# A two-layer graph-attention kernel: Q, K and V of a group computed one step later, the start of the kernel laid out anew, and a bias added elsewhere

## Chip, core and metric

The kernel runs on one core of one Trainium2 chip. The metric is the device time of one execution in microseconds (us). Names of engines: PE is the matrix engine (PEld its weight loads), DVE the vector engine, ACT the scalar engine, POOL the GpSimd engine, SP the engine that issues nearly all DMAs here. Each engine works through its own queue in order.

## What is computed

There are 128 graphs of 128 nodes with 512 features, `x[128,128,512]`, and an adjacency matrix `adj[128,128,128]` of zeros and ones for each. All is float32. Layer 0 is masked attention with 8 heads of 64 features and an output projection, layer 1 a graph attention with one head whose softmax runs over the other axis:

```python
q, k, v = x @ Wq + bq, x @ Wk + bk, x @ Wv + bv            # (128, 128, 512) each
a = softmax(where(adj > 0, q_h @ k_h.T / 8, -1e9))         # for each of 8 heads
x = layernorm(x + relu(concat_h(a @ v_h) @ Wo + bo))
Wh = x @ W                                                 # layer 1
e = leaky(Wh @ a[:512] + (Wh @ a[512:]).T, 0.2)            # (128, 128) for each graph
att = softmax(where(adj > 0, e, -9e15), axis=1)
out = layernorm(x + leaky(att @ Wh, 0.2))
```

bk has no effect on a softmax over the keys and is not used by the kernel.

## The kernel before

**Products.** Every large product is cut into 2 x 2 blocks and done by Winograd's form of Strassen's scheme (`strassen`): seven block products p1, p5, p6, p2, p7, p4, p3 in place of eight. Right-hand blocks (weights) are summed once at the start by four DVE subtractions (`right_blocks`, L134-137), left-hand blocks for each product by four POOL operations (`left_blocks`, L289-292). Three PSUM accumulators y, w, x take the seven products: p1, p6, p7, p4 go into y, and ACT reads y out after p1 (t0), p6 (t2), p7 (t3) and p4, before the next product adds to it; p5 and p3 go into w, with a DVE addition that needs t3 between them; p2 goes into x, and DVE adds t0 to it.

**Groups.** Q, K and V are computed for a group of four graphs at once (`products`, `group_product`): 3 x 7 = 21 block products of 8 matmul instructions on line 361 (tiles st_y, st_w, st_x), in a fixed order in which the three chains overlap. Three PSUM banks "a", "b", "c" are handed from chain to chain, so a first use of a bank by one chain waits until the chain before has read it out. The sums of V's weights are written to DRAM once and fetched into a ring of three buffers for each group (wv_n, L402). Wo and W1 are used for pairs of graphs (`project_o` in odd steps, `project_w` in even ones, L442, tiles p_y, p_w, p_x).

**Steps.** The order on all five engines is written by hand: a loop over steps t (one graph each) issues the scores of graph t (lg, L486, 16 matmuls), its softmax (DVE maxima L495 and L501, eight exponentials L507 and eight divisions L521 on ACT), a round trip through DRAM and a DVE transpose (paT, L536), the attention product of graph t-1 (p_oT, L549) and its copy to SBUF (L561), the projections of earlier graphs, and layer 1 of graph t-7. `group()` is called five times in a step, after the maxima, after the transpose, after the first four divisions, after the attention product, and at the end; each call issues one of the 21 products (the last call of the fourth step what is left). So the products fill PE while the softmax runs on ACT and DVE.

**Before the first scores.** The loop begins at t = -4. Before it the kernel loads the bias rows (L110, L111, on ACT's queue) and turns them (L114-116), loads graphs 0 to 3 one by one with four DMAs each (L257, on SP's queue), Wq in 16 DMAs (ACT's queue), Wk and Wv in 16 each (SP's), scales Wq's four blocks (L151), and transposes the graphs (L262); the last transpose of a group also issues the POOL sums xS. Group g's products are issued in steps 4g-4 to 4g-1, so those of group 0 in steps -4 to -1, where nothing else runs.

**Wo and W1.** Wo is loaded in step 0 and combined in one piece at the end of step 1: the four subtractions, then `bo_b` += bv @ Wo by ten PE products (p_bo, L184-189), and the split of the bias row into three bf16 rows (L197-204). W1 is loaded in step 2 and combined at the end of step 4: 16 dot products with the attention vector on DVE (wa_scr, L229), eight tiny additions (L240) and the four subtractions.

Of the kernel before, what the change touches and what calls it, by code (L numbers as in the profile page):

```python
# [8 lines left out]
F32 = mybir.dt.float32  # L9
# [8 lines left out]
GROUP = 4  # L18
EPS = 1e-5
# [5 lines left out]
def kernel(  # L25
# [16 lines left out]

# [67 lines left out]
    nc.scalar.dma_start(b_rows[:NC, :], bq.rearrange("(c p) -> c p", p=P))  # L110
    nc.scalar.dma_start(b_rows[NC:, :], bv.rearrange("(c p) -> c p", p=P))  # L111
    b_cols = const.tile([P, 2, NC], F32, name="b_cols")
    p_b = psum("p_b")
    nc.tensor.transpose(p_b[:, : 2 * NC], b_rows, ident[: 2 * NC, : 2 * NC])  # L114
    nc.vector.tensor_scalar_mul(b_cols[:, 0, :], p_b[:, :NC], QSCALE)
    nc.vector.tensor_copy(b_cols[:, 1, :], p_b[:, NC : 2 * NC])

    def weight_blocks(w, t, queue, spread_rows=True):

        b12 = work.tile([P, 2, t[0].shape[-1]], F32, name="b12", tag="z")  # L120
        blocks = {(0, 0): t[0], (1, 0): t[1], (0, 1): b12, (1, 1): t[2]}
        for (k, o), dst in blocks.items():
            if spread_rows:
                rows = w.rearrange("(q k c i) (o f) -> k o q i c f", q=4, k=2, c=2, o=2)
                for q in range(4):
                    queue.dma_start(dst[32 * q : 32 * q + 32, :, :HALF], rows[k, o, q])
            else:
                rows = w.rearrange("(k c p) (o f) -> k o p c f", k=2, c=2, o=2)
                queue.dma_start(dst[:, :, :HALF], rows[k, o])
        return blocks  # L130

    def right_blocks(t, b12):

        nc.vector.tensor_sub(t[4], b12, t[0])  # L134
        nc.vector.tensor_sub(t[6], t[2], b12)
        nc.vector.tensor_sub(t[5], t[2], t[4])
        nc.vector.tensor_sub(t[3], t[1], t[5])
# [7 lines left out]
    def load_wq():  # L145
        t = [wq[:, n] for n in range(7)]
        blocks = weight_blocks(Wq, t, nc.scalar)

        def combine():
            for dst in blocks.values():  # L150
                nc.vector.tensor_scalar_mul(dst, dst, QSCALE)  # L151
            right_blocks(t, blocks[0, 1])

        return combine

    def load_wk():
        t = [wk[:, n] for n in range(7)]
        blocks = weight_blocks(Wk, t, nc.sync)
        return lambda: right_blocks(t, blocks[0, 1])

    def load_wv():
        tiles = [big.tile([P, 2, 2, HALF], F32, name="wv_t", tag="v", bufs=3) for _ in range(3)]
        tiles.append(work.tile([P, 2, 2, HALF], F32, name="wv_t", tag="paT"))
        t = [tiles[n // 2][:, n % 2] for n in range(7)]
        blocks = weight_blocks(Wv, t, nc.sync)

        def combine():
            right_blocks(t, blocks[0, 1])
            for n in range(7):
                nc.sync.dma_start(wv[n], t[n])  # L170

        return combine

    def load_wo():

        t = [wo[:, n] for n in range(7)]
        blocks = weight_blocks(Wo, t, nc.sync, spread_rows=False)
        bo_b = work.tile([P, D], F32, name="bo_b", tag="y")
        nc.sync.dma_start(bo_b, bo.partition_broadcast(P))

        def combine():
            right_blocks(t, blocks[0, 1])
            rows = work.tile([P, NC, P], F32, name="bv_rows", tag="z")
            nc.vector.tensor_copy(rows, b_cols[:, 1, :].unsqueeze(2).to_broadcast([P, NC, P]))  # L184
            p = psum("p_bo")
            parts = [(0, 0, 0), (0, 1, 1), (1, 0, 0), (1, 4, 0), (1, 2, 1)]
            for o, n, k in parts:
                for c in range(2):
                    nc.tensor.matmul(
                        p[:, o * HALF : (o + 1) * HALF],  # L190
                        rows[:, 2 * k + c, :],
                        wo[:, n, c, :],
                        start=o == 0 and n == 0 and c == 0,
                        stop=True,
                        skip_group_check=True,
                    )
            nc.vector.tensor_add(bo_b, bo_b, p)  # L197
            nc.vector.tensor_sub(bo_b[:, HALF:], bo_b[:, HALF:], bo_b[:, :HALF])
            for n in range(3):
                row = slice(32 * n, 32 * n + 1)  # L200
                part = work.tile([P, D], BF16, name="b_part", tag="z")
                nc.vector.tensor_copy(part, bo_b)
                nc.vector.tensor_copy(bias_rows[row, :], part[row, :])
                nc.vector.tensor_sub(bo_b, bo_b, part)

        return combine

    bias_rows = const.tile([96, D], BF16, name="bias_rows")
    nc.gpsimd.memset(bias_rows, 0.0)
    ones = const.tile([96, P], BF16, name="ones")  # L210
    nc.gpsimd.memset(ones, 1.0)

    def load_w1():

        t = [w1[:, n] for n in range(7)]
        blocks = weight_blocks(W1, t, nc.sync)
        a_b = work.tile([P, 2, D], F32, name="a_b", tag="x1T")
        nc.sync.dma_start(
            a_b.rearrange("p s f -> p (s f)"),
            a1.rearrange("f o -> (f o)").partition_broadcast(P),  # L220
        )

        def combine():
            sums = small.tile([P, 2, 2, 2, 2], F32, name="wa", bufs=1)
            for (k, o), block in blocks.items():
                for c in range(2):
                    for s in range(2):
                        scr = work.tile([P, HALF], F32, name="wa_scr", tag="y")
                        nc.vector.scalar_tensor_tensor(  # L229
                            scr,  # L230
                            block[:, c, :HALF],
                            1.0,
                            a_b[:, s, o * HALF : (o + 1) * HALF],
                            op0=ALU.mult,
                            op1=ALU.mult,
                            accum_out=sums[:, s, k, o, c : c + 1],
                        )
            for (k, o), block in blocks.items():
                for c in range(2):
                    nc.vector.tensor_add(  # L240
                        block[:, c, HALF:],
                        sums[:, o, k, 0, c : c + 1],
                        sums[:, o, k, 1, c : c + 1],
                    )
            right_blocks(t, blocks[0, 1])

        return combine
# [19 lines left out]
    def load_x(b):  # L267
        X[b] = spread(x[b])
# [6 lines left out]
    def transpose_x(b):  # L275
# [4 lines left out]
        if j == GROUP - 1:  # L280
            sums = big.tile([P, 3, 2, 2 * P], F32, name="xS")
            XS[g] = left_blocks(XT[g], sums)
# [100 lines left out]
    def products(g):  # L383
# [20 lines left out]
        def fetched(n):  # L404
# [4 lines left out]
            group_product(g, 3 * g, lambda n: wq[:, n], features_first(Q), True, b_cols[:, 0, :]),  # L409
            group_product(g, 3 * g + 1, lambda n: wk[:, n], features_first(K), True),  # L410
# [10 lines left out]
        order = chains[0][:5]  # L421
        for n in range(3):
            if n < 2:
                order.append(chains[n + 1][0])
            order += chains[n][5:]
            if n < 2:
                order += chains[n + 1][1:5]
        return order

    def pair_product(xs, w, add, bias=None):  # L430
# [3 lines left out]
        def multiply(p, n, start):  # L434
# [6 lines left out]
            for kc in range(2):  # L441
# [3 lines left out]
                    w[:, n, kc, :],  # L445
# [95 lines left out]
    def attend(sm):  # L541
# [16 lines left out]
        def copy():  # L558
            if h == 0:
                OT[pair] = work.tile([P, NC, 2 * P], F32, name="oT")  # L560
            nc.scalar.copy(OT[pair][:, :, h * P : (h + 1) * P], p)  # L561
# [157 lines left out]
    combine = {}  # L719
    group_steps = []  # L720
    later = []
    sm = fin = none

    x_turns = [(8,), (8, 9), (9,), ()]
    load_x(0)
    load_x(1)
    combine["wq"] = load_wq()
    load_x(2)
    load_x(3)
    transpose_x(0)  # L730
    transpose_x(1)
    combine["wq"]()
    combine["wk"] = load_wk()
    transpose_x(2)
    transpose_x(3)
    load_x(4)
    combine["wk"]()
    combine["wv"] = load_wv()
    for t in range(-4, B + 9):
        pair_steps = []  # L740
        if t % GROUP == 0 and on(t + 4):
            group_steps = products((t + 4) // GROUP)
# [5 lines left out]
        def group(n=1):  # L748
            for _ in range(min(n, len(group_steps))):
                group_steps.pop(0)()  # L750

# [4 lines left out]
        if on(t + 1):  # L756
            load_mask(t + 1)
        if t == 0:
            combine["wo"] = load_wo()
        if t == 2:  # L760
            combine["w1"] = load_w1()
# [11 lines left out]
        fin.stats()  # L773
        pair()
# [34 lines left out]
        if t == 4:  # L809
            combine["w1"]()  # L810
# [7 lines left out]
        if t == -4:  # L818
            combine["wv"]()
        if t == 1:  # L820
            combine["wo"]()
        group(21 if t % GROUP == GROUP - 1 else 1)
# [41 lines left out]
```

## Time and profile before

| what | value |
|---|---|
| median of 3 runs | 2527.51 us (2526.45 to 2529.57) |
| the profiled execution | 2527.99 us, span of its trace 2526.2 us |
| busy in it: PE, DVE, ACT, POOL | 2445.9, 1809.8, 1355.3, 801.6 us |
| granted PE clock, mean | 0.985 |
| 4 steps in the middle (1000.00 to 1075.30 us) | PE 75.30, DVE 55.41, ACT 42.22, POOL 25.03 us busy |
| scores of step 0 to 6 begin at | 57.64, 68.60, 91.01, 104.59, 124.18, 135.32, 164.47 us |
| scores of step 124 to 127 begin at | 2386.19, 2400.69, 2416.73, 2434.21 us |

In the profile a group of instructions is named by its line, engine and operation and by the tiles that it writes and reads ("st_y<-xT,wq"). The timeline gives start, duration, and in brackets the time for which the engine sat idle before and what released it. The table of waits gives for each waiting engine and line the total, the number and the longest wait.

### The profile page before, as it was taken

How to read it: one execution, taken by the hardware profiler on the slowest of the kernel's cores; microseconds unless marked ns; L12 is line 12 of the kernel's file. 1: busy time of each engine (PE TensorE's matmuls, PEld its weight loads, DVE VectorE, ACT ScalarE, POOL GpSimd, SP SyncE). 2: the span in 40 equal slices, each digit the busy share in tenths (PEclk: the TensorE clock that was granted, in tenths of full speed). 3: DMA queues.
4: the chain of work that ended last, by engine and by line, in shares of the span. 5: the costliest groups of instructions: out<-in, count | busy, mean ns of one | idle time of the engine just before them, and what ended most of it. 6: DMA issues, size and time to landing. Idle time of an engine off the chain costs nothing.

```text
span 2526.2 us, 43418 instructions
## 1 busy us (share of the span) xinstructions
PE 2445.9 (97%) x13717; PEld 2009.6 (80%) x13717; DVE 1809.8 (72%) x3758; ACT 1355.3 (54%) x4801; POOL 801.6 (32%) x1161
## 2 busy tenths in 40 slices
PE   7889999999999999999999999999999999999975
PEld 6778888888888888888888888888888888888753
DVE  4567777777777777777777777777777777777675
ACT  1445555555565565565555555555555555555541
POOL 1132333332333332333333233333233333233232
PEclk9999999999999999999999999999999999999987
DMA  5544554545554545445545444545445545444441
GB/s 169 154 133 150 156 151 157 158 145 162 155 153 150 162 148 158 153 150 159 157 153 159 148 153 152 160 154 157 147 155 153 159 154 155 154 153 147 145 132 46
DMA packets 353350, 379.91 MB, mean 150 GB/s; under 512 B 39640, under 2 KB 257760, under 8 KB 353120
## 3 DMA queue, kind: packets, MB, share of 16 engines
q1 hardware_dynamic: 351824, 376.07, 47.9%
q8 instruction: 110, 1.80, 0.3%
q10 hardware_dynamic: 1296, 1.05, 0.2%
q14 instruction: 120, 0.98, 0.1%
HBM read 240.91 MB, written 136.05 MB: 149 GB/s over the span
## 4 chain that ended last, share of the span: by engine, by line
PE 93%; DVE 3%; ACT 1%; DMA 1%; issue 1%; POOL 0%; SPq 0%; DVEq 0%; ACTq 0%; POOLq 0%
PE st_y L361 26%; PE p_y L442 17%; PE st_w L361 13%; PE p_w L442 8%; PE st_x L361 7%; PE lg L486 5%; PE p_oT L549 5%; PE p_h L683 4%; PE p_x L442 4%; ACT pa L507 1%; PE p_e L654 1%; PE p_e L655 1%; DVE pa L495 0%; DVE wa_scr L229 0%; DVE z L692 0%
## 5 line engine op out<-in xcount | busy, mean ns | idle before, releaser
L575 POOL TENSOR_SCALAR ve<-mv 128x1 f32<-128x1 f32 x256 | 68.7, 268 | 1187.8 <-DVE mv L572 1187.8
L507 ACT ACTIVATE pa<-pa,nmax 128x128 f32<-128x128 f32 x1024 | 400.4, 393 | 25.7 <-DVE nmax L501 22.6
L521 ACT ACTIVATE pa<-pa,rs 128x128 f32<-128x128 f32 x1024 | 333.1, 396 | 0.1
L495 DVE TENSOR_TENSOR pa<-lg,mf 128x512 f32<-128x512 f32 x256 | 164.7, 685 | 71.2 <-PE lg L486 69.1
L338 ACT COPY st_t<-st_y 128x512 f32<-128x512 f32 x192 | 110.4, 575 | 186.7 <-PE st_y L361 186.7
L643 DVE TENSOR_TENSOR wh<-p_w,pr_t 128x257 f32<-128x257 f32 x128 | 54.5, 426 | 211.2 <-ACT pr_t L453 125.1
L486 PEld LDWEIGHTS lg<-kT,qT 64*128 64x128 f32 x2048 | 124.2, 187 | 93.7 <-issue 93.7
L507 ACT ACTIVATION_READ_ACCUMULATOR pa<-pa,nmax 128x1 f32 x1024 | 194.8, 190 | 0.0
L577 POOL TENSOR_TENSOR rstd<-ve,mhalf 128x1 f32<-128x1 f32 x256 | 176.8, 691 | 21.4
L453 ACT COPY pr_t<-p_y 128x256 f32<-128x256 f32 (+1 forms) x384 | 140.8, 367 | 76.8 <-PE p_y L442 76.1
L342 ACT ACTIVATE st_t<-st_y,b_cols 128x256 f32<-128x256 f32 x192 | 80.6, 470 | 177.2 <-PE st_y L361 177.2
L687 ACT COPY z<-p_h 128x512 f32<-128x512 f32 x128 | 75.1, 586 | 181.9 <-PE p_h L683 167.4
L289 POOL TENSOR_TENSOR oS<-oT 128x256 f32<-128x256 f32 x64 | 46.8, 731 | 396.1 <-ACT oT L561 396.1
L536 DVE STREAM_TRANSPOSE paT<-paz 128x1024 f32<-128x1024 f32 x128 | 159.4, 1245 | 4.9 <-DMA paz<-pa_dram 4.2
L501 DVE TENSOR_REDUCE nmax<-pa 128x8 f32<-128x1024 f32 x128 | 156.2, 1220 | 4.4
L561 ACT COPY oT<-p_oT 128x512 f32<-128x512 f32 x128 | 75.1, 586 | 154.9 <-PE p_w L442 151.9
L683 PE MATMUL p_h<-wh,att 128*128 128x512 f32 x256 | 134.0, 605 | 17.5 <-DVE att L674 17.5
L549 PEld LDWEIGHTS p_oT<-paT,v 128*64 128x64 f32 x2048 | 113.4, 140 | 46.3 <-issue 34.5
L486 PE MATMUL lg<-kT,qT 64*128 64x128 f32 x2048 | 148.7, 285 | 0.0
L442 PE MATMUL p_y<-w,x1S 128*128 128x257 f32 x512 | 134.6, 385 | 13.8 <-ACT pr_t L453 13.8
L549 PE MATMUL p_oT<-paT,v 128*64 128x128 f32 x2048 | 144.9, 285 | 1.8 <-DVE rs L517 1.8
L442 PE MATMUL p_y<-wo,oS 128*128 128x256 f32 x512 | 134.5, 386 | 10.2 <-ACT pr_t L453 10.2
(154 smaller groups left out, 6027.0 us busy)
## 6 DMA issues: line engine op xcount, KB each, us to landing
pa_dram<-pa SPq DMA_DIRECT2D x128, 512.0 KB, 2.6
paz<-pa_dram SPq DMA_DIRECT2D x512, 128.0 KB, 2.9
wv_n<-wv SPq DMA_DIRECT2D x224, 256.0 KB, 2.9
xz<-in_x_dram SPq DMA_DIRECT2D x512, 64.0 KB, 2.4
x<-in_x_dram SPq DMA_DIRECT2D x128, 256.0 KB, 3.1
x_dram<-x SPq DMA_DIRECT2D x128, 256.0 KB, 2.3
xz<-x_dram SPq DMA_DIRECT2D x512, 64.0 KB, 2.0
out_dram<-z SPq DMA_DIRECT2D x128, 256.0 KB, 2.0
```

Of the source, the lines that this page charges most:

```text
L361: nc.tensor.matmul(p[:, m, :], lhs, rhs, start=start and m == 0 and kc == 0, stop=True, skip_group_check=True,)
L442: nc.tensor.matmul(p[:, :width], xs[n][:, kc, :], w[:, n, kc, :], start=start and kc == 0, stop=True, skip_group_check=True,)
L453: nc.scalar.copy(t[:, :width], p[:, :width])
L486: nc.tensor.matmul(self.lg[r][:, c, :], q[rows, c, cols], k[rows, c, cols], start=True, stop=True)
L495: nc.vector.tensor_add(by_head[:, r * NC : (r + 1) * NC], self.lg[r].rearrange("p c (b k) -> p c b k", b=4), mf.unsqueeze(1).to_broadcast( ...
L501: nc.vector.tensor_reduce(self.nmax, by_head, AX.XY, ALU.max, negate=True)
L507: nc.scalar.activation(self.pa[:, :, h, :], self.pa[:, :, h, :], AF.Exp, bias=self.nmax[:, h : h + 1], accum_out=self.sums[:, h : h + 1],)
L521: nc.scalar.activation(self.pa[:, :, h, :], self.pa[:, :, h, :], AF.Copy, scale=self.rs[:, h : h + 1])
L536: nc.vector.transpose(self.paT.rearrange("p h (a i) -> p a h i", i=32), self.paz.rearrange("p a (h k) -> p a h k", k=32),)
L549: nc.tensor.matmul(p[r * HD : (r + 1) * HD, c, :], v[:, h * HD : (h + 1) * HD], sm.paT[:, r * NC + c, :], start=True, stop=True,)
L577: nc.gpsimd.tensor_tensor(rstd, ve, mhalf, ALU.pow)
L683: nc.tensor.matmul(p.rearrange("p (o f) -> p o f", o=2), edge.att, wh, start=True, stop=True)
```

## The change

- `products(g)` starts at t = 4g-3 in place of 4g-4, and the loop begins at t = -3. Products 1 to 15 (Q and K whole and V's p1) are issued in the three steps before the group's first scores, V's p5, p6, p2, p7, p4, p3 in the step of those scores. In each chain p3 now comes ahead of p4; in group 0 the first chain runs p1, p2, p5, p6, p7.
- The POOL sums of group g+1 (`sum_x`) are issued early in step 4g. Graphs are loaded and transposed at other steps (`x_turns`), as many in four steps as before.
- Graphs 0 to 3 come as two pairs of four DMAs each and two transposes of 1024 columns; weight blocks in 8 DMAs in place of 16; the blocks have other places in memory (`PLACE`). The bias rows are issued on ACT's queue after Wq, and their PE transpose still stands ahead of the first product.
- bv is added to O^T when it is copied out of PSUM: four activations with a bias column in place of one copy. The product p_bo and what fed it are gone.
- The sums of Wk, Wv, Wo, the bias rows and W1 are a list of small operations ("chores"); each `group()` call issues two after its product. Wo is loaded in step -2, W1 in step -1.

```diff
-            nc.scalar.copy(OT[pair][:, :, h * P : (h + 1) * P], p)
+            for c in range(NC):
+                nc.scalar.activation(
+                    OT[pair][:, c, h * P : (h + 1) * P],
+                    p[:, c, :],
+                    AF.Identity,
+                    bias=b_cols[:, 1, c : c + 1],
+                )
...
-        order = chains[0][:5]
-        for n in range(3):
-            if n < 2:
-                order.append(chains[n + 1][0])
-            order += chains[n][5:]
-            if n < 2:
-                order += chains[n + 1][1:5]
-        return order
+        order = [chains[0][n] for n in ((0, 3, 1, 2, 4) if g == 0 else range(5))]
+        for n in range(2):
+            order += [chains[n + 1][0], chains[n][6], chains[n][5]]
+            order += chains[n + 1][1:5]
+        return order + chains[2][5:]
...
-    x_turns = [(8,), (8, 9), (9,), ()]
...
+    x_turns = [(), (7, 8), (8,), (8,)]
+    xz = load_pair(0, "pa")
+    load_blocks(Wq, columns(wq), nc.scalar)
+    nc.scalar.dma_start(b_rows[:NC, :], bq.rearrange("(c p) -> c p", p=P))
+    nc.scalar.dma_start(b_rows[NC:, :], bv.rearrange("(c p) -> c p", p=P))
+    xz2 = load_pair(1, "paz")
+    load_blocks(Wk, columns(wk), nc.sync)
+    XT[0] = big.tile([P, NC, GROUP * P], F32, name="xT")
...
+    wq_sums = right_blocks(places(wq))
+    scale(0)
+    transpose_pair(0, xz)
+    scale(1)
+    transpose_pair(1, xz2)
+    sum_x(0)
+    scale(2)
+    wq_sums[0]()
+    scale(3)
+    for op in wq_sums[1:]:
+        op()
+    turn_biases()
     load_x(4)
-    combine["wk"]()
-    combine["wv"] = load_wv()
-    for t in range(-4, B + 9):
+    load_x(5)
+    chores += right_blocks(places(wk)) + load_wv()
+    for t in range(-3, B + 9):
         pair_steps = []
-        if t % GROUP == 0 and on(t + 4):
-            group_steps = products((t + 4) // GROUP)
+        if t % GROUP == 1 and on(t + 3):
+            group_steps = products((t + 3) // GROUP)
...
             for _ in range(min(n, len(group_steps))):
                 group_steps.pop(0)()
+            for _ in range(min(CHORES, len(chores))):
+                chores.pop(0)()
...
-        if t == 0:
-            combine["wo"] = load_wo()
-        if t == 2:
-            combine["w1"] = load_w1()
+        if t == -2:
+            load_blocks(Wo, columns(wo), nc.sync, spread_rows=False)
+            more_chores = right_blocks(places(wo)) + load_bias()
+        if t == -1:
+            chores += more_chores
+            more_chores = load_w1()
+        if t == 0:
+            chores += more_chores
...
         fin.stats()
+        if t % GROUP == 0 and on(t + GROUP):
+            sum_x(t // GROUP + 1)
...
-        group(21 if t % GROUP == GROUP - 1 else 1)
+        group(21 if t % GROUP == 0 else 1)
```

`CHORES` is 2. `load_wv` gives as chores one write of a block to DRAM, the four subtractions and six more writes; `load_bias` one subtraction and three splits of three operations; `load_w1` eight pairs of dot products, four pairs of tiny additions and the four subtractions.

## Prediction

> **What bounds the kernel now.** I read the page's chain first, then busy time by stretches, then the waits and the timeline of the first 165 us, and last the end.
>
> ```profile
> PE 93%; DVE 3%; ACT 1%; DMA 1%; issue 1%; POOL 0%; SPq 0%; DVEq 0%; ACTq 0%; POOLq 0%
> ```
>
> The chain runs over PE. Busy time of PE, PEld, DVE, ACT, POOL for four steps early on and in the middle:
>
> ```profile
> 76.80:152.10 75.30, 64.46 (x364) 52.73 (x364) 50.32 (x116) 30.98 (x113) 16.43 (x20) 0.95 0.50 149
> 1000.00:1075.30 75.30, 75.30 (x429) 62.21 (x429) 55.41 (x116) 42.22 (x151) 25.03 (x37) 1.00 0.49 154
> ```
>
> In the middle PE never idles: four steps cost 75.3 us, 18.8 each, whatever the other engines do. Time can only be won before about 165 us, where PE waits, and after 2387. PE's waits of the first 200 us:
>
> ```profile
> PE st_w L361 <- POOL xS L289: 6.6, 1, 6.6
> PE st_w L361 <- DVE qT L379: 5.2, 1, 5.2
> PE st_y L361 <- DMA b<-in_L_gnn_Wq_dram: 5.0, 1, 5.0
> PE p_bo L189 <- DVE bv_rows L184: 3.2, 1, 3.2
> ```
>
> The first PE product starts at 8.3, the second only at 18.7 (behind scaling and sums of Wq, transposes, POOL's xS). Then 19 more run, and the scores of step 0 begin at 57.64. Step 1 takes 22.4 us (68.60 to 91.01) because Wo's lump of DVE and PE work stands in it, step 5 takes 29.2 (135.32 to 164.47) because W1's lump (135.0 to 147.1 on DVE) stands ahead of its maxima:
>
> ```profile
> 83.08 6.27 PE L189 MATMUL p_bo<-wo,bv_rows 128*128 128x256 f32 x20 [3.17 <-DVE bv_rows L184]
> 149.01 3.46 PE L361 MATMUL st_w<-xT,wq 128*128 128x256 f32 x8 [5.20 <-DVE qT L379]
> ```
>
> Prices from rows: a block product 1.73 us (the chain's pitch), scores 1.09, p_oT 1.03, project_o 6.3, project_w 6.1, a DVE sum 0.60, a bias part 1.44, an exponential with its accumulator 0.58, a division 0.295, an ACT copy of a bank 0.59.
>
> **Part 1, to the first scores.** The PE queue begins with the transpose of the bias rows, which now follow Wq's 8 DMAs. By issue alone (0.57 us each, then 1.64 to land) they are there at 7.9. By bytes they come later: ahead of them lie 2 MB (graphs 0 to 3 and Wq), and before moved at most 230 to 242 GB/s in the slices from 4.5 to 9 us, so some 10. I take 10 (bounds 7.9 and 12, the latter by the mean pace to 10.5 us). The page's DMA row for this, of the first 60 us in slices of 1.5:
>
> ```profile
> GB/s 0 133 173 233 230 242 161 231 132 135 142 145 141 131 138 137 136 159 134 133 131 199 378 407 365 325 170 124 150 160 15 0 75 124 150 216 180 262 249 289
> ```
>
> [...]
>
> From 10: p1 cold 3.7 (the row before: 8 matmuls in 3.78), p2 and p5 1.73 each, p6 to 18.9. p5's inputs (POOL's first sum, 1.27 after pair 1's transpose, and one sum of Wq) are due at about 12.5, so the wait of 6.6 goes. Next late is ACT's reading of p6 (0.84 plus hand-over), on which p7 now follows directly: 1.1. p7 ends at 21.8, K's p1 at 23.5. Q's p3 needs p7's DVE addition, and that stands behind Wv's first sums in DVE's queue; Wv is the last of 4.5 MB, there at about 20.8 (240 GB/s and 2 us to land); three sums and two transposes later it is 24.0, the addition 24.7. So p3 starts at 24.8: a wait of 1.3. Q's p4, 28.2; K's p5 waits 1.0 for ACT's copy of p4 (same bank), ends 31; six more products: 41.4. **Scores of step 0 at 41.5** (bounds 39 and 48: a start at 7.9, or Wv and the writes of its sums, which share SP's queue with the fetches, late by 6). That is 16.1 earlier, 10.4 of it because six products are left over.
>
> **Part 2, steps 0 to 5.** The six products of V now stand in steps 0 and 4, where no project_o or project_w fills PE, and they hang on ACT: p7 on the copy of p6, which comes after six exponentials, p4 on the copy of p7, which comes after all divisions. From the scores' end: maxima 2.6, exponentials 3.5, copy 0.6, p7; then two exponentials, eight divisions, cast and copy to 11.4; p4, p3, next scores: 16.2. In step 0 the maxima also stand behind two bias parts, a transpose and a mask (2.6 late): 18.9 us where step 0 before had 10.96. In step 4 bv's activations come before the copy (1.2): 17.3 plus 0.5, where it had 11.1. Each time PE idles some 4 us. Rows on that: after an idle time of 2.17 the next 8 matmuls took 1.99, after 5.20 they took 3.46. The Trainium skill, "TensorE: Matmul & The Clock Gate", section "The HAM clock gate", puts the fall to half rate at an idle window of about 3.4 us; by it each of these gaps would cost up to 1.7 more, by the shorter row nothing. I count 0.5 for step 4, and nothing for step 0, where ACT is later than even a half-rate p7.
>
> Step 1 is like step 0 before: 11.2, as the rest of W1's chores is under 4 us of DVE. Step 2 has Q's p4, then K's p5 on the same bank behind exponentials and four divisions: 14.3. Step 3: 18.3, step 5: 17.8, by PE's work. Sum 18.9 + 11.2 + 14.3 + 18.3 + 17.8 + 17.8 = 98.3 where it was 106.8. **Scores of step 6 at 139.8 in place of 164.47: 24.7 won.** Step 7 has one product less than before: 26.4.
>
> **Part 3, the middle.** p_oT's copy becomes four activations. Nearest rows: one copy of 512 columns 0.586, one activation of 128 from PSUM 0.368, two of 256 in 0.84; so 1.2, 0.6 more in a step, ACT 42 to 45 of 75. It is off PE's path if the hand-overs keep their slack. The two that get tight are Q's p4 to K's p5 in step 4g+2 and K's p4 to V's p5 over the end of step 4g+3 (1.4 us left, by the order of ACT's queue). For the first, ACT's read of the product before and PE's start of the next in such a step:
>
> ```profile
> 2321.14 0.84 ACT L342 ACTIVATE st_t<-st_y,b_cols 128x256 f32<-128x256 f32 x2 [0.67 <-PE st_y L361]
> 2322.93 1.99 PE L361 MATMUL st_x<-xT,wq 128*128 128x256 f32 x8
> ```
>
> 0.9 us is left. K's p3 to the next scores has 4.4 us of other PE work for 0.7 of DVE. POOL's sums (5.1 us) start at about 8 us of step 4g, done before O^T's at 13.8. SP issues as many DMAs in four steps as before. So nothing; bounds 0 and 0.5 us a group each at the two places.
>
> **Part 4, the end.** Step 124 gets the six products that step 0 of the kernel shed. Before it took 14.5, with
>
> ```profile
> 2394.26 1.74 PE L442 MATMUL p_y<-w,x1S 128*128 128x257 f32 x4 [3.06 <-ACT pr_t L453]
> ```
>
> and now costs a full step with V's products, 20.2 (step 123 before: 2365.97 to 2386.19): 5.7 lost. ACT's 0.6 on the last graphs' way to project_o: 0.6 more.
>
> **The sum.** 26.4 - 5.7 - 0.6 = 20.1. The profiled execution's span 2526.2 becomes 2506.1, its 2527.99 us 2507.9; the median shown lies 0.5 below the profiled time, so I say **2508**. A measurement here can tell about 0.2% (5 us) from no change.
>
> **Rivals.** (a) *The V steps stall less and PE starts early*: scores of step 0 at 39, steps 0 and 4 at 13 each, since DVE may get to the maxima sooner: 2.5 + 5.9 + 4.8 more, 2495. For it: only step 0 has the backlog. Against: ACT's order is fixed, and the exponentials before p6's copy alone are 3.5. 0.14. (b) *The start is late*: V's weights go through SP in order with writes, x, Wo and W1, and each wait there holds all behind it; scores of step 0 at 48 and step 0 longer by 3 to 5: 2518. For it: before, SP's queue stood behind the ring of V for 9 us at 42.9. Against: nothing in the new order needs the ring before V's p1. 0.13. (c) *Slower: ACT becomes the bound at the hand-over*. If ACT is as late at the third `group()` as in the steps that have K's p2, where its read began 11.0 us after the scores' start and PE's next product at 12.1, a read of 0.84 leaves 0.2, and bv's 0.6 a step eats that. It decides from 20 / 31 = 0.65 us a group; at 1.0 a group it is 31 us: 2539. Against: ACT idles 33 of 75 us and catches up in each step. 0.08. (d) *It nets out*: (b) with some of (c), about 2526. 0.05. The forecast has 0.60.
>
> **Chances and range.** Faster by over 0.2%: 0.60 + 0.14 + 0.13 = 0.87; within: 0.05; slower: 0.08. The range takes in (a) and (b), 2495 to 2521.
>
> **What would show it.** Right: scores of step 0 near 41.5 and of step 6 near 140; no p_bo; steps 0 and 4 at 16 to 19 with PE idle for ACT's st_t; four steps in the middle still 75.3; step 124 at about 20. Wrong: PE waits on line 361 in the middle (c), a wait on wv_n or on Wv's sums of over 3 us in the first 60 (b), steps 0 and 4 under 14 (a).

## The result and the profile after

The changed kernel takes **2584.74 us** (median of 4 runs, 2582.17 to 2592.98); four runs of the kernel before beside it have a median of 2528.44. The ratio is 1.0229 [1.0203, 1.0255]: slower, where 2508 was predicted. The profiled execution took 2592.98 us, its span is 2589.9 us, 63.7 more than before, at a granted clock of 0.983 (before 0.985). It is the slowest of the four: the medians differ by 56.3 us, so the 63.7 that are taken apart below are more than the usual loss.

The first place to look is the page's chain of waits, shares of the span by engine. PE had 93% of it before:

```profile
PE 67%; DVE 12%; DMA 8%; issue 4%; SPq 3%; ACT 3%; POOL 1%; DVEq 0%; POOLq 0%; ACTq 0%
```

DMA had 1% of that chain and SP's queue 0%; now they have 8% and 3%. Busy time of PE, PEld, DVE, ACT, POOL over 500 us of the middle, where PE had been busy without a gap:

```profile
1000.00:1500.00 500.00, 488.61 (x2747) 400.96 (x2746) 359.90 (x745) 289.58 (x1044) 154.67 (x232) 0.99 0.46 149
```

PE idles 11.4 of 500 us, all through the middle, while DVE, the busiest of the other engines, works 72% of the time: nothing is saturated, so it must be a hand-over. PE's waits (total, number, longest) name it:

```profile
PE st_x L354 <- DMA wv_n<-wv: 55.3, 31, 6.5
...
PE p_b L114 <- DMA b_rows<-in_L_gnn_bv_dram: 13.7, 1, 13.7
PE st_w L354 <- ACT qT L335: 7.6, 30, 1.6
```

Line 354 is the product line (361 before). Its st_x reads V's weights for p2, once a group, and 31 of 32 groups wait there for the fetch from DRAM. The last row is a second, smaller wait of 30 groups, K's p5 on ACT's copy of Q's p4.

**Where the 63.7 us come from**, by the starts of the scores (us):

| scores of step | 0 | 1 | 2 | 3 | 4 | 5 | 6 | 8 | 124 | end |
|---|---|---|---|---|---|---|---|---|---|---|
| before | 57.64 | 68.60 | 91.01 | 104.59 | 124.18 | 135.32 | 164.47 | 201.92 | 2386.19 | 2526.2 |
| after | 48.92 | 69.31 | 80.45 | 94.66 | 112.07 | 134.28 | 151.69 | 187.41 | 2444.96 | 2589.9 |

At step 8 the new kernel leads by 14.5 us, at step 124 it is 58.8 behind, at the end 63.7. So the start won 14.5, the 29 groups between lost 73.3 (2.53 each), the end lost 4.9. Mean length of a step in the middle (steps 8 to 119, by t mod 4 = 0, 1, 2, 3): before 18.30, 18.49, 18.30, 20.22, together 75.3; after 22.20, 18.49, 18.56, 18.49, together 77.7. V's last products moved from class 3 to class 0, which should have given 20.03, 18.49, 18.30, 18.49: the same 75.3. Class 0 lies 2.17 above that, class 2 lies 0.26 above. The last group lost more than the others, as its step 120 took 25.58.

**Why the fetch is late.** V's blocks stream through a ring of three buffers: each product of V also issues a fetch, on SP's queue, and the fetch issued with p5 brings the block of p2. SP's queue in a step 4g of the changed kernel (start, duration, line, tiles), whose scores began at 1040.71:

```profile
1041.64 0.34 SPq L594 DMA_DIRECT2D x_dram<-x  x1
1042.02 0.43 SPq L456 DMA_DIRECT2D adj<-in_adj_dram  x1
1042.95 0.32 SPq L594 DMA_DIRECT2D x_dram<-x  x1
1043.68 3.67 SPq L239 DMA_DIRECT2D xz<-x_dram  x8
1047.45 0.38 SPq L395 DMA_DIRECT2D wv_n<-wv  x1
```

and in the step of the kernel before that holds the same fetch, step 119, whose scores began at 2290.65:

```profile
2288.14 1.74 SPq L532 DMA_DIRECT2D paz<-pa_dram  x4
2289.92 0.43 SPq L465 DMA_DIRECT2D adj<-in_adj_dram  x1
2290.45 0.38 SPq L402 DMA_DIRECT2D wv_n<-wv  x1
```

In the old place the fetch goes out 0.2 us before the scores. In the new place it goes out 6.7 us after them, since the program puts it behind the two stores of x1 (which wait for DVE's normalisation) and the eight spreads that read x1 back (xz, 3.67 us to issue). Those stand at the head of even steps only. V's p5 stood in an odd step and was moved to an even one. Landing takes as long as before (median 2.9 us in both), so the weights arrive some 7 us later against the same products. Where a store is late the fetch is later still: in step 8, whose scores began at 187.41, it went out at 196.01, 8.6 us after them. PE in step 52, the one shown first, and in steps 8 and 4 (brackets: idle time before, and what ended it):

```profile
1050.14 1.99 PE L354 MATMUL st_x<-wv_n,xT 128*128 128x256 f32 x8 [0.93 <-DMA wv_n<-wv]
...
198.84 3.44 PE L354 MATMUL st_x<-wv_n,xT 128*128 128x256 f32 x8 [2.92 <-DMA wv_n<-wv]
...
123.40 3.60 PE L354 MATMUL st_x<-wv_n,xT 128*128 128x256 f32 x8 [6.51 <-DMA wv_n<-wv]
```

In 7 of the 31 groups the product itself then takes 3.4 to 3.8 us in place of 2.0, mostly after the longer waits (the last section has the exceptions). So a group between steps 8 and 119 pays more (2.17) than its wait (1.58 in the mean).

**The head.** From the timeline of the changed kernel's first 25 us, with the engines side by side:

```profile
0.72 7.48 ACTq L124 DMA_DIRECT2D wq<-in_L_gnn_Wq_dram  x8
0.72 7.58 SPq L272 DMA_DIRECT2D xz<-in_x_dram  x8
...
9.77 0.27 ACTq L727 DMA_DIRECT2D b_rows<-in_L_gnn_bv_dram  x1
...
13.70 0.24 PE L114 MATMUL p_b<-ident,b_rows 8*128 8x8 f32 x1 [13.70 <-DMA b_rows<-in_L_gnn_bv_dram]
...
14.53 1.64 DVE L136 TENSOR_TENSOR wq<-wq 128x512 f32<-128x512 f32 x1
...
21.53 0.15 DVE L116 COPY b_cols<-p_b 128x4 f32<-128x4 f32 x1
...
21.69 1.28 ACT L335 ACT_TABLE_LOAD   x1 [21.69 <-DVE b_cols L116]
...
22.98 0.84 ACT L335 ACTIVATE st_t<-st_y,b_cols 128x256 f32<-128x256 f32 x2
...
23.92 3.40 PE L354 MATMUL st_y<-xS,wq 128*128 128x256 f32 x8 [2.84 <-issue]
```

The bias rows gate PE until 13.7, and again ACT's first read (t0, hence p6 at 23.92), because they are turned on DVE only after all sums of Wq, three of which took 1.64 us.

### The profile page after: what moved, and what is told of

Same layout as the page of the kernel before. It is cut to its first block, busy times and chain, and to the rows that moved or that the text cites. A ratio compares the mean times of both kernels' runs of the same rounds, so it can differ in the third digit from the quotient of the medians.

```text
span 2589.9 us, 43731 instructions
## 1 busy us (share of the span) xinstructions
PE 2457.6 (95%) x13697; PEld 2007.5 (78%) x13697; DVE 1815.5 (70%) x3754; ACT 1440.9 (56%) x5185; POOL 777.7 (30%) x1161
## 4 chain that ended last, share of the span: by engine, by line
PE 67%; DVE 12%; DMA 8%; issue 4%; SPq 3%; ACT 3%; POOL 1%; DVEq 0%; POOLq 0%; ACTq 0%
PE st_y L354 18%; PE p_y L433 12%; PE st_w L354 10%; PE st_x L354 7%; PE p_w L433 6%; PE p_oT L540 4%; PE lg L477 4%; DMA wv_n<-wv 3%; SPq L239 3%; PE p_h L680 3%; DMA x_dram<-x 3%; DVE st L567 3%; PE p_x L433 2%; DVE x L586 2%; DVE xT L244 2%
## 5 line engine op out<-in xcount | busy, mean ns | idle before, releaser
L512 ACT ACTIVATE pa<-pa,rs 128x128 f32<-128x128 f32 x1024 | 339.4, 394 | 42.8 <-DVE rs L508 42.8
L553 ACT ACTIVATE oT<-p_oT,b_cols 128x128 f32<-128x128 f32 x512 | 146.0, 368 | 208.5 <-PE p_w L433 203.6
L486 DVE TENSOR_TENSOR pa<-lg,mf 128x512 f32<-128x512 f32 x256 | 164.5, 684 | 102.4 <-PE lg L477 98.2
L372 DVE TENSOR_TENSOR v<-st_w,st_t 128x512 f32<-128x512 f32 x64 | 44.3, 692 | 144.1 <-ACT st_t L331 85.3
L654 ACT ACTIVATE e<-p_e,wh 128x128 f32<-128x128 f32 x128 | 47.3, 370 | 161.3 <-PE p_e L652 161.3
```

The lines of the kernel that those rows point to most:

```text
L486: nc.vector.tensor_add(by_head[:, r * NC : (r + 1) * NC], self.lg[r].rearrange("p c (b k) -> p c b k", b=4), mf.unsqueeze(1).to_broadcast( ...
L512: nc.scalar.activation(self.pa[:, :, h, :], self.pa[:, :, h, :], AF.Copy, scale=self.rs[:, h : h + 1])
L553: nc.scalar.activation(OT[pair][:, c, h * P : (h + 1) * P], p[:, c, :], AF.Identity, bias=b_cols[:, 1, c : c + 1],)
```

## The experiments

The theory: **queue order**. The move of V's products put the fetch for their p2 behind x1's stores and spreads on SP; it costs 2.2 us a group, some 65 us, and nothing else in the change is slower by much. Rivals: **ACT**, whose four bias activations delay every hand-over; and **the moved order itself**, slow wherever the fetch stands. The kernel before, beside these runs, had medians of 2527.72 (runs 1 to 4), 2526.9 (5 to 8) and 2527.43 (9 and 10).

**1. The fetch issued earlier.** V's block for p2 is fetched with K's p4, at the end of the step before, and not with V's p5.

```diff
         def fetched(n):
-            fetch()
+            if n != 4:
+                fetch()
             return ring.pop(n)
...
+        last_of_k = chains[1][5]
+
+        def with_next_fetch():
+            last_of_k()
+            fetch()
+
+        chains[1][5] = with_next_fetch
```

> V's second block (for p2) is fetched with K's p4 at the end of step 4g+3 in place of with V's p5 in the next step; the ring keeps three buffers, every other fetch stays. Queue theory: in the changed kernel that fetch stands on SP's queue behind the eight spreads of x1 and their wait for x_dram, so steps 4g+4 take 22.2 in place of 20.0; without that the wait of st_x for wv_n (55.3 us) goes, steps 4g+4 go to 20.0 to 20.1, 31 x 2.2 = 67 us are won: about 2518 (2512 to 2524). ACT theory (bv's activations make ACT late, and the wait for the fetch only stands where PE would wait anyway): the wait moves to ACT's copies and the time stays within 15 us of 2585.

Measured: 2526.12 us (11 runs, 2521.14 to 2528.35), ratio 0.999 [0.9981, 0.9999]; 58.6 less than the change. PE's waits:

```profile
PE st_w L354 <- ACT qT L335: 7.5, 30, 1.6
...
PE st_y L354 <- DMA wv_n<-wv: 4.5, 4, 3.2
```

The wait of 55.3 is gone (0.7 is left of it), class 0 falls from 22.20 to 20.08, the other three stay. One fetch's place in a queue made the whole distance to the kernel before. The 7.5 on qT remain, and the end is as in the change. The 67 us that were expected came from the changed kernel's trace, its slowest execution; run 1's trace is 68.4 shorter than that one, its median 58.6 lower. Step 4 still waits 3.2 us for a later block.

**2. bv left out.** O^T is copied by one plain copy, so the output lacks the term bv.

```diff
-            for c in range(NC):
-                nc.scalar.activation(
-                    OT[pair][:, c, h * P : (h + 1) * P],
-                    p[:, c, :],
-                    AF.Identity,
-                    bias=b_cols[:, 1, c : c + 1],
-                )
+            nc.scalar.copy(OT[pair][:, :, h * P : (h + 1) * P], p)
```

> O^T is copied out by one plain copy as before; bv is left out of the computation (its values are zeros in the inputs). All else as in the changed kernel. ACT theory: the waits go with the 0.55 us of ACT work a step, the time falls by 40 us or more. Queue theory: st_x's wait for wv_n stays at 45 to 65 us; at most the wait of K's p5 for ACT's copy qT (7.6 us in total) goes, 2575 to 2590. If that wait stays too, it is not bv's activations but DVE, behind whose queue the maxima and so the exponentials of that step are late.

Measured: 2590.27 us (4 runs), ratio 1.0249 [1.0236, 1.0263]. PE's waits:

```profile
PE st_x L354 <- DMA wv_n<-wv: 53.7, 31, 6.3
...
PE st_w L354 <- ACT qT L335: 7.4, 30, 1.6
```

Both are as they were. The ACT rival falls: the 0.6 us of ACT a step are hidden, and the qT wait isn't theirs either.

**3. Only the shift undone.** Q, K and V at their old steps; pairs, chores, bias columns and the order within a chain as changed.

```diff
-    x_turns = [(), (7, 8), (8,), (8,)]
+    x_turns = [(8,), (8, 9), (9,), ()]
...
-    for t in range(-3, B + 9):
+    for t in range(-4, B + 9):
...
-        if t % GROUP == 1 and on(t + 3):
-            group_steps = products((t + 3) // GROUP)
+        if t % GROUP == 0 and on(t + 4):
+            group_steps = products((t + 4) // GROUP)
...
-        group(21 if t % GROUP == 0 else 1)
+        group(21 if t % GROUP == GROUP - 1 else 1)
```

(The POOL sums and the load of graph 5 go back to their old places with it.)

> Only the shift is undone: products start at t = 4g-4, the loop at t = -4, the graphs are transposed at the steps of before, POOL's sums follow the last transpose. Pairs, biases' place, bv in O^T, chores and the order p3 before p4 stay as changed. Queue theory: no wait for wv_n, four steps in the middle 75.3; first scores about 10 us later than in the changed kernel (six products), 59; no V products without cover in steps 0 and 4, no lump in steps 1 and 5, the end as before: 2508 to 2518. ACT theory: bv's activations are still there, so the middle stays above 76.5 and the time above 2555.

Measured: 2512.93 us (5 runs), ratio 0.9933 [0.992, 0.9947]. The middle is 18.30, 18.49, 18.30, 20.22 again, without a wait. So the rest of the change is worth 14.8 us, and the shift costs some 72, of which the fetch's place is 58.6 (run 1). It isn't worth having with the fetch mended either: against run 1, this kernel's first scores are 15.8 us later (62.84 against 47.06) but its step 8 only 3.4 (187.68 against 184.30), it gains 8.6 over the 29 groups and 4.0 at the end. One wait is new here, in step 1, where Q's p4 and K's p5 now follow each other on one PSUM bank:

```profile
86.02 3.61 PE L354 MATMUL st_w<-xS,wk 128*128 128x256 f32 x8 [2.93 <-ACT qT L335]
```

**4. The spreads issued later.** The ring is as changed, and x1's eight spreads are issued after the step's first product.

```diff
         def spread_both():
-            store(0)
             for h in (1, 0):
                 X[2 * pair + h, 1] = spread(d[h])
...
-                    later.append(spread_both)
+                    later.append(lambda: store(0))
+                    last_of_all.append(spread_both)
...
         group()
+        while last_of_all:
+            last_of_all.pop(0)()
```

> The ring's order is left as changed; instead the eight spreads of x1 are issued after the first group call of the step, so V's fetch stands ahead of them on SP's queue (and behind the two writes of x1). Queue theory: the fetch is issued some 4 us earlier, the wait for wv_n goes or falls under 5 us, 2515 to 2528; x1's spreads land about 0.5 us later, which nobody waits for until the end of the step. A theory that the transfer itself is slow (traffic at that time): the fetch lands later than 2.9 us after its issue and the time stays above 2550.

Measured: 2521.69 us (8 runs), ratio 0.9972 [0.9962, 0.9982]; class 0 at 20.14. What is left of the wait:

```profile
PE st_x L354 <- DMA wv_n<-wv: 2.3, 1, 2.3
```

Runs 1 and 4 move different DMAs, the fetch and what stood ahead of it, and remove the same wait. What counts is the order of the two on the queue.

**5. The bias rows first** on ACT's queue, turned before Wq is scaled, on top of run 1.

```diff
+    nc.scalar.dma_start(b_rows[:NC, :], bq.rearrange("(c p) -> c p", p=P))
+    nc.scalar.dma_start(b_rows[NC:, :], bv.rearrange("(c p) -> c p", p=P))
     load_blocks(Wq, columns(wq), nc.scalar)
-    nc.scalar.dma_start(b_rows[:NC, :], bq.rearrange("(c p) -> c p", p=P))
-    nc.scalar.dma_start(b_rows[NC:, :], bv.rearrange("(c p) -> c p", p=P))
...
+    turn_biases()
     scale(0)
...
-    turn_biases()
```

> With the early fetch, the bias rows are issued on ACT's queue ahead of Wq, and turned before Wq is scaled. The first product then waits for Wq's first column and pair 0 alone and starts at 9.5 to 10.5 in place of 13.9, and p6 no longer waits for the bias columns behind Wq's sums on DVE. DVE theory: the sums of Wk and Wv and the transposes of the next graphs stand in DVE's queue ahead of what Q's p3 needs, and they take as long as before, so only 2 to 3 us arrive at the first scores: 2522 to 2524. Start theory: the 4 us and p6's wait arrive whole: 2518 to 2521.

Measured: 2523.13 us (11 runs), ratio 0.9983 [0.9974, 0.9992]. PE's first product starts at 9.47 in place of 14.55, and p6 at 17.90 in place of 23.50, so the place of the bias rows costs some 5 us there. Q's p3 then waits 2.69 us for DVE, and the first scores come at 44.12 in place of 47.06, those of step 8 at 179.84 in place of 184.30. The first scores of kernels that are the same up to there differ by as much (47.06 in run 1, 50.10 in run 9), and the medians differ by 3.0, with runs that scatter by 7 to 10 us; so how much of the 5 us reaches the end is not shown.

**6. Q's p4 ahead of its p3**, on top of run 1, to test whether the order of the change makes the qT wait.

```diff
-            order += [chains[n + 1][0], chains[n][6], chains[n][5]]
+            ends = (5, 6) if n == 0 else (6, 5)
+            order += [chains[n + 1][0]] + [chains[n][m] for m in ends]
```

> With the early fetch, Q's p4 comes ahead of its p3 again as in the kernel before (K's p3 stays ahead of p4). The wait of K's p5 for ACT's copy of Q's p4 stands 30 times, 7.5 us in all, whether or not bv is added on ACT. Order theory: it is there because p4 is now the product just before p5 on the same bank; with p4 one call earlier it goes, four steps take 75.3 in place of 75.6, 2517 to 2520. Theory that ACT is late in that step whatever the order: the wait moves to another product or stays, 2524 to 2528.

Measured: 2525.72 us (11 runs), ratio 0.9988 [0.9979, 0.9997]. The qT wait left the list, yet class 2 is still 18.61: 0.3 us moved to the projection (1.96 us from start to start ahead of its p7, where 1.73 is the pitch). This theory fell. It looks as if ACT is late in that step whatever the order, which run 9 takes up.

**7 and 8. Without the shift: Q's order (8), and the bias rows first as well (7).** The edits are those of runs 3, 6 and 5.

> Without the shift, Q's p4 ahead of p3. Order theory: the wait in step 1 (2.93 us, then 8 matmuls in 3.6 in place of 2.0) and the one of 0.9 before the first scores go; in the middle nothing was lost: 2507 to 2510. If ACT is late there whatever the order: 2512 to 2514.

> Without the shift, Q's p4 ahead of p3, and the bias rows first. Against the run without the shift: step 1 loses its wait of 2.9 us for ACT's copy and the cold matmuls behind it (4 to 5 us), as in the run with the order alone, and the start wins 2 to 4 us more: 2503 to 2508.

Measured: 2507.13 us (5 runs), ratio 0.992 [0.9907, 0.9932], and 2503.79 (4 runs), 0.9905 [0.9892, 0.9919]. Without the shift the order does matter: step 1 takes 12.3 us where it took 17.0 in run 3, and in run 8 the first scores come at 58.27 (run 3: 62.84). In run 7 PE's first product starts at 9.27 (13.90 in run 8), but the first scores only at 59.18, since a new queue wait ate it. SP's queue in run 7:

```profile
34.91 0.43 SPq L395 DMA_DIRECT2D wv_n<-wv  x1
35.38 0.43 SPq L457 DMA_DIRECT2D adj<-in_adj_dram  x1
35.85 7.07 SPq L124 DMA_DIRECT2D w<-in_L_gnn_W_dram  x8
43.16 0.35 SPq L194 DMA_DIRECT2D a_b<-in_L_gnn_a_dram  x1
43.72 9.44 SPq L395 DMA_DIRECT2D wv_n<-wv  x4
```

and PE's product behind it:

```profile
49.42 3.38 PE L354 MATMUL st_x<-wv_n,xT 128*128 128x256 f32 x8 [4.78 <-DMA wv_n<-wv]
```

The same cause a second time: W1's eight loads, which DVE first reads at 62.84, stand ahead of V's fetch. At steps 8 and 124 run 7 is 0.9 us later than run 8; its trace is 6.2 us shorter, and the medians differ by 3.3, by what comes after step 124, where the two programs are the same. So the 3.3 us are not shown to come from the bias rows; the last section says what differs there.

**9. The maxima first.** On top of run 1, each step's maxima precede x1's last normalisation and store.

```diff
+        sm.maxima()
         while later:
             later.pop(0)()
-        sm.maxima()
```

> With the early fetch (Q's p3 ahead of p4 as changed), the step's maxima stand ahead of the normalising of x1 (which waits for POOL) in DVE's queue. In step 4g+2 the maxima begin 1.6 us after the scores' end, behind two normalisings and Q's last addition, which the shift brought to the end of an odd step; ACT's exponentials and divisions follow late, and PE loses 0.25 us to ACT in each group whatever the order of Q's products. DVE theory: the maxima begin 0.9 us or more earlier, ACT's copy is in time, steps 4g+2 take 18.30 in place of 18.55, about 8 us won: 2516 to 2520. If DVE's order is not the cause: 2524 to 2528.

Measured: 2536.82 us (7 runs), ratio 1.0031 [1.002, 1.0043]: a miss in the time, and it tells the cause of the qT wait. DVE in such a step of the change, whose scores ended at 1004.75:

```profile
1004.64 0.52 DVE L578 TENSOR_SCALAR x<-x,mv,rstd 128x512 f32<-128x512 f32 x1
1005.07 0.68 DVE L372 TENSOR_TENSOR qT<-st_w,st_t 128x512 f32<-128x512 f32 x1
1005.93 0.55 DVE L578 TENSOR_SCALAR x<-x,mv,rstd 128x512 f32<-128x512 f32 x1 [0.17 <-POOL rstd L574]
1006.39 1.28 DVE L486 TENSOR_TENSOR pa<-lg,mf 128x512 f32<-128x512 f32 x2
```

and in run 9, whose scores ended at 988.11:

```profile
988.42 0.68 DVE L372 TENSOR_TENSOR qT<-st_w,st_t 128x512 f32<-128x512 f32 x1
989.03 1.28 DVE L494 TENSOR_TENSOR pa<-lg,mf 128x512 f32<-128x512 f32 x2
```

The maxima (L486, there L494) start 1.6 us after the scores in the change and 0.9 after them here. Class 2 is 18.30 again: DVE's order before the maxima made ACT late, and K's p5 waited for it. But x1's second store now comes later on SP (4.2 us after the start of the scores in steps 4g and 5.0 in steps 4g+2, where run 1 has 2.5 and 3.1), the spreads too, and V's next fetches stand behind them:

```profile
PE st_y L354 <- DMA wv_n<-wv: 18.5, 19, 4.4
```

Class 0 rises from 20.08 to 20.52, more than class 2 gave back: 6.1 us over the 29 groups. The first scores come 3.0 later as well, but the program is that of run 1 up to there, so this is the difference of two executions.

**10. Both lessons together**: no shift, Q's order, the bias rows first, run 1's early fetch, and W1's load one step later. The last edit:

```diff
         if t == -1:
             chores += more_chores
-            more_chores = load_w1()
         if t == 0:
+            more_chores = load_w1()
+        if t == 1:
             chores += more_chores
```

> Without the shift, Q's p4 ahead of p3, bias rows first, and in addition the early fetch of V's block and W1's load one step later. In the run without these two, V's p2 of group 0 waits 4.8 us for its block, which stands on SP's queue behind the nine DMAs of W1. Queue theory: that wait and the cold matmuls after it go, first scores at 53 to 54 in place of 59.2, 2496 to 2500. If the transfers themselves are slow there: 2502 to 2505.

Measured: **2499.98 us** (4 runs, 2498.93 to 2503.09), ratio 0.9892 [0.9877, 0.9906]: 27 us under the kernel before and 85 under the change. The first scores come at 53.00, those of step 8 at 175.92 (run 7: 180.06), and the middle is

```profile
1000.00:1500.00 500.00, 500.00 (x2841) 412.95 (x2840) 372.90 (x767) 294.12 (x1071) 161.40 (x236) 1.00 0.48 155
```

with PE never idle.

## Why the prediction was wrong, step by step

**The step that failed: Part 3**, "SP issues as many DMAs in four steps as before. So nothing". The count is right, the conclusion is not. The six products were moved with their fetches from an odd step to an even one, and what stands ahead of them on SP's queue differs between the two. The prediction had named SP's queue as what holds all behind it, in rival (b), but only for the first 60 us. The signal it gave for (b), "a wait on wv_n", did come, in 31 of 32 groups, but all after the first 60 us to which it was tied; and PE's wait on the product line in the middle, its signal for (c), came without (c)'s cause. The price of the fetch's new place was to be had from before's trace: in even steps the spreads take 3.66 us to issue, behind two stores, so a fetch behind them goes out some 6 us after the scores and lands 3 later. The product that needs it stands 8.5 us after the scores (2290.65 to 2299.20). That gives a loss of about a microsecond in the best group, and more where a store or a landing is late. The spreads of before in step 118, whose scores began at 2272.35:

```profile
2275.00 3.66 SPq L257 DMA_DIRECT2D xz<-x_dram  x8
```

Measured: 2.17 a group over steps 8 to 119 and 5.55 in step 120, together 66 of the 73.3 us that the 29 groups between steps 8 and 124 lost.

**Part 3, the hand-over Q's p4 to K's p5**: bounds 0 and 0.5 us a group, 0 taken, 0.26 measured (class 2), some 7 over these groups. Rival (c) had this place and the wrong cause: ACT is late because DVE starts the maxima late (run 9), and bv's activations cost nothing (run 2). That part of Part 3, bv's price of 0, was right.

**Part 1**: scores of step 0 at 41.5 predicted, 48.92 measured, just beyond the bound of 48. Of the 7.4 us, 3.9 are p1's start (13.9 for 10, and beyond the bound of 12): the bias rows stood behind eight weight DMAs that took 0.95 us each to issue and not 0.57, so the second of them went out at 9.77, and it was there at 13.7. Another 2.8 are p6 (10.0 after p1 in place of 7.2), held by the bias columns behind DVE's sums and by ACT's table load of 1.28. From p6 to the scores 24.3 were predicted and 25.0 measured. Run 5, which takes the biases away from both, starts p1 at 9.47 and p6 at 17.90 (17.2 predicted) and has the first scores at 44.12; there Q's p3 waits 2.69 for DVE where 1.3 was predicted.

**Part 2**, steps 0 to 5, predicted and measured: 18.9 and 20.4, 11.2 and 11.1, 14.3 and 14.2, 18.3 and 17.4, 17.8 and 22.2, 17.8 and 17.4. Four of six are right within 1 us. Step 4 is long by V's fetches, the wait of 6.51 shown above; with that one fetch earlier (run 1) PE waits 3.2 us for a later block and the step still takes 22.1, with the spreads later (run 4) 19.1. The start won 14.5 where 26.4 was predicted: 7.4 of the 11.9 missing are in the first scores, 5.9 in steps 0 and 4, and 1.4 came back elsewhere.

**Part 4**: 5.7 + 0.6 lost was predicted. Measured 4.9: step 124 took 21.15 where it was 14.50, that is 6.65 lost, and the steps behind it gave 1.7 back. The sum's last line takes off nothing for the 0.5 that it names: 2507.9 less 0.5 is 2507.4 and not 2508.

With the measured terms the sum is 14.5 - 73.3 - 4.9 = -63.7, the whole difference of the spans. Even with Part 3 at nothing, the shift would hardly have paid: of the 15.8 us that run 1 wins over run 3 ahead of the first scores, 3.4 are left at step 8, and 4.0 are lost at the end.

## What to carry to other kernels

A queue that issues in order is a schedule of its own: when work is moved to another step, write out what stands ahead of each of its DMAs there, with the waits of those DMAs, and compare when the data is needed; a count of DMAs per period says nothing. A fetch from DRAM that waits for nothing should be issued ahead of stores and reloads that wait for an engine. A pipeline's start that is shortened by moving work into the steps behind it is judged by a later step, here step 8, not by its first product: 15.8 us at the first scores were 3.4 at step 8.

## What the runs showed of the hardware

**Idle time and the matrix engine's speed.** The last steps hold the same idle time of 3.06 us in two kernels, and the four matmuls after it differ by a factor of nearly two. Run 8:

```profile
2371.28 2.05 PE L434 MATMUL p_y<-w,x1S 128*128 128x257 f32 x4 [3.06 <-ACT pr_t L445]
```

Run 7:

```profile
2372.20 1.11 PE L434 MATMUL p_y<-w,x1S 128*128 128x257 f32 x4 [3.06 <-ACT pr_t L445]
```

In steps 76 and 100 of the change PE had worked for over 8 us without a gap before it fell idle, and there it even goes against the length of the idle time:

```profile
1519.01 3.50 PE L354 MATMUL st_x<-wv_n,xT 128*128 128x256 f32 x8 [1.91 <-DMA wv_n<-wv]
...
1988.51 1.99 PE L354 MATMUL st_x<-wv_n,xT 128*128 128x256 f32 x8 [3.44 <-DMA wv_n<-wv]
```

The granted clock over the first product is 0.55, over the second 1.00. The Trainium skill, "TensorE: Matmul & The Clock Gate", section "The HAM clock gate", has the half rate come after an idle window of about 3.4 us. Here it came after 1.91 and stayed away after 3.44, so between these the idle time just before does not decide it; what does, no run here shows. The end of this kernel varies with it: another four matmuls took 2.05 us in run 8 and 1.11 in run 7 after the same 2.83, and from the scores of step 127 to the end run 7 took 91.1 us, run 8 94.7. Whether this is also what scatters the runs of one kernel by 7 to 11 us (runs 1, 5, 6, 9) stays open, as each has one trace.

**Issue times.** DMAs of double the rows took 0.95 us each to issue at the start, on both queues (7.48 and 7.58 for eight), where the smaller ones of before took 0.57 to 0.60. Halving their number saved little there. It is not the size alone: eight of the same size took 4.95 us for Wk, from 9.14 on, and 3.75 for Wv, from 17.98.

**DVE beside POOL.** Three of Wq's sums took 1.64 us while POOL formed xS (each POOL sum 1.35 to 1.60), and 0.68 once POOL was done.
